# Mixture-of-experts tiles moved between the attention rounds of later blocks

## The chip, the cores and the metric

The kernel runs on one core of a Trainium2 chip. The metric is device time in microseconds (us): the median of three runs. One further execution was taken with the hardware profiler; all views below are of that execution.

## What is computed

The input is 16 sequences of 256 tokens of width 128, in float32. Four residual layers follow each other: causal attention with 16 heads of width 8, a mixture of experts, a second attention (no mask, another scaling of the scores), and the same mixture of experts again.

```python
x = x + attn_a(layernorm(x))
x = x + ffn(layernorm(x))
x = x + attn_b(layernorm(x))
x = x + ffn(layernorm(x))

def ffn(x):                       # 8 experts, 2 per token, hidden width 512
    top_vals, top_idx = top_k(x @ Wr, 2)
    rw = softmax(top_vals)
    combine = sum(rw[..., None] * one_hot(top_idx, 8))
    h = silu(x @ Wg[e]) * (x @ Wu[e])
    eo = (h @ Wd[e]) / sqrt(12)
    return sum over e of combine[:, e] * eo[:, e]
```

Both attentions take a softmax over the keys, so they need exponentials; the experts need a SiLU.

## The kernel before

**Two attentions, each followed by its experts.** The 4096 tokens are cut into 8 blocks of 512 tokens (two sequences of 256). `attention` goes over 128 rounds. A round is one block, one sequence of it, and one of 8 pairs of head groups: two heads at a time. At round `at` the loop emits, in this order: the scores of that round with queries on the partitions (`rows_scores`), the exponentials of the round 14 rounds back (`exponentials`: the scores again with keys on the partitions, then Exp on ScalarE, and for the causal layer a POOL select on the diagonal), the mask and the row maxima (`rows_maxima`: one VectorE reduction), and every second round the product with the values of the round 17 back (`values`). The maxima are transposed and laid into two spare rows of q by a DMA (`lay_maxima`), so that the second scores come out with the maximum subtracted.

**Everything else is cut into tasks.** `project` (layer norm, q, k, v of a block), `collect` (division by the sum), `finish` (output projection and residual) and `route` are generators. At each `yield` a task names in how many rounds it wants to go on and what it needs: `BANK` (the one PSUM bank for small products, tag `mm`), `BUSY` (a busy engine) or `FREE`. `later` and `due` give out at most one or two such steps after each round. All engine calls of this part go through `InOrder`, which keeps the program order on each engine.

**Routing.** `route` takes a finished block, normalizes it, computes the expert logits, finds the best two, counts with two small matmuls which place each token gets in its expert's region of the DRAM table `rows_in` (`free` carries the counts from block to block), and scatters each token's row twice with 8 indirect DMAs from POOL, one per round. A row is 128 values, the token's number and its weight.

**Experts.** After the last block `tiles_of` turns the counts into a list of 39 tiles of 256 rows (expert number and first row each), `pads` fills the open end of each region with 8 DMAs, and `experts` runs over the 39 tiles. The order of this part is left to the scheduler. A tile loads its rows and three weight matrices (`fetch`, 0.9 MB, all on SP's queue), transposes the rows, and in four steps of 128 hidden units multiplies by Wg and Wu, takes Silu on ScalarE and the product on VectorE; then it multiplies by Wd (`down`), scales by the token's weight, and adds the 256 result rows to DRAM sums with two indirect DMAs from POOL that accumulate (`finish`). The adds alternate between two sums, and adds to one sum follow one another. Tokens of a tile that do not exist are sent to a spare row. After the second layer the two sums are loaded, added and stored.

**Buffers.** q and k have three buffers of a whole block each (`qs`, `ks`), v has three with 32 columns per head of which 9 are used. PSUM has 8 banks: in attention three pairs for the scores (`psum_s`), one for the values and one for small products.

The lines that set the pace of the experts' stage:

```python
    experts("a", attention(weights_a, True, "a"), totals[0], False)
    experts("b", attention(weights_b, False, "b"), totals[1], True)
```

Of the kernel before, what the change touches and what calls it, by code (L numbers as in the profile page):

```python
# [32 lines left out]
F32 = mybir.dt.float32  # L34
# [8 lines left out]
P = 128  # L43
NH = 16
# [12 lines left out]
SEQ = 256  # L57
EPS = 1e-5
# [4 lines left out]
TOKENS = 4096  # L63
W = P + 2
# [6 lines left out]
def layers(  # L71
# [23 lines left out]
    ot = out.flatten_outer_dims().rearrange("(n t p) d -> n p t d", t=NT, p=P)  # L95
# [18 lines left out]
    def attention_weights(wq, bq, wk, bk, wv, bv, wo, bo, scale, name):  # L114
# [27 lines left out]
    blocks = ctx.enter_context(tc.tile_pool(name="blocks", bufs=4))  # L142
# [17 lines left out]
    half = const.tile([P, NE], F32, name="half")  # L160
# [14 lines left out]
    tokens = const.tile([P, NB * NT], F32, name="tokens")  # L175
    within = tokens[:, 0:ET]
    nobody = const.tile([P, 1], F32, name="nobody")
# [4 lines left out]
    totals = [  # L182
        [dram.tile([TOKENS + P, P], F32, name=f"total{i}{j}") for j in range(2)] for i in range(2)
    ]
    blank = const.tile([P, 3 * W], F32, name="blank")
    wr_sb = const.tile([P, NE], F32, name="wr_sb")

    def zeros():

        yield sy.dma_start(  # L190
            out=rows_in[NE * CAP : NE * CAP + TE, :].rearrange("(s p) d -> p s d", p=P),
            in_=blank[:, 0 : ET * W].rearrange("p (s d) -> p s d", s=ET),
        )
        for first, second in totals:
            flat = second.rearrange("(p a m) d -> p a (m d)", p=P, m=3)
            for k, m in ((0, 4), (4, 8), (8, 11)):
                to = flat[:, k:m, :]
                yield sy.dma_start(
                    out=to,
                    in_=blank[:, 0 : 3 * P].unsqueeze(1).to_broadcast([P, to.shape[1], 3 * P]),  # L200
                )
            yield sy.dma_start(out=first[TOKENS : TOKENS + P, :], in_=blank[:, 0:P])

    slots = [const.tile([P, 2, NT], I32, name=f"slots{n}") for n in range(NB)]

    vs = [const.tile([P, NT, NH, HS], F32, name=f"v{i}") for i in range(3)]
    qs = [const.tile([P, NP, TB], F32R, name=f"q{i}") for i in range(3)]
    ks = [const.tile([P, NP, TB], F32R, name=f"k{i}") for i in range(3)]
# [30 lines left out]
    def later_constants():  # L239
# [19 lines left out]
        for t, pattern, base, by_partition in (  # L259
# [4 lines left out]
            (tokens, [[P, NB * NT]], 0, 1),  # L264
            (nobody, [[0, 1]], TOKENS, 1),
# [8 lines left out]
    def prepared(i):  # L274

        for t in (ks, qs) if i else ():
            for g in range(0, NP, 4):
                po.memset(t[i].bitcast(F32)[:, g : g + 4, :], 0.0)
                yield 1, FREE
        for j in range(2):  # L280
            row = j * HP + TOP
            sy.dma_start(
                out=ks[i].bitcast(F32)[row : row + 2, :, :].rearrange("p g (a m) -> p (g a) m", m=P),
                in_=ones[0:2, :].unsqueeze(1).to_broadcast([2, NP * NT, P]),
            )
        po.memset(vs[i], 0.0)
        po.memset(vs[i].rearrange("p t h r -> p (t h) r")[:, :, 0:1], 1.0)
# [44 lines left out]
    def route(pool, psum, n, xb, free, sent):  # L332
# [4 lines left out]
        yield 1, BUSY  # L337
# [6 lines left out]
            tokens[:, n * NT : (n + 1) * NT].unsqueeze(1).to_broadcast([P, 2, NT]),  # L344
# [54 lines left out]
        ve.tensor_tensor(w2, share[:, 1], w1, ALU.mult)  # L399
        for t in range(NT):  # L400
            for s in range(2):
# [6 lines left out]
                tc.declare_no_dep(scatter.ins, group=sent[0], reason="no row is written twice")  # L408
                tc.add_to_no_dep_group(sent[0], scatter.ins)
                sent.append(scatter)  # L410

    def tiles_of(pool, free):

        count = pool.tile([P, NE], F32, tag="count")
        nc.vector.tensor_tensor(count, free, regions, ALU.subtract)
        more = pool.tile([P, NE, CAP // TE], F32, tag="more")
        nc.vector.tensor_tensor(
            more, count.unsqueeze(2).to_broadcast([P, NE, CAP // TE]), steps, ALU.is_gt  # L420
        )
        need = pool.tile([P, NE], F32, tag="need")
        nc.vector.tensor_reduce(need, more, AX.X, ALU.add)
        sums_to = pool.tile([P, NE, NE], F32, tag="sums_to")
        nc.vector.tensor_tensor(
            sums_to, need.unsqueeze(1).to_broadcast([P, NE, NE]), upto, ALU.mult
        )
        end = pool.tile([P, NE], F32, tag="end")
        nc.vector.tensor_reduce(end, sums_to, AX.X, ALU.add)
        wide = [P, TILES, NE]  # L430

        past = pool.tile([P, TILES, NE + 1], F32, tag="past")
        nc.vector.memset(past[:, :, 0:1], 1.0)
        nc.vector.tensor_tensor(
            past[:, :, 1:], numbers.unsqueeze(2).to_broadcast(wide),
            end.unsqueeze(1).to_broadcast(wide), ALU.is_ge,
        )
        expert = pool.tile([P, TILES], F32, tag="expert")
        nc.vector.tensor_reduce(expert, past[:, :, 1:], AX.X, ALU.add)
        mine = pool.tile(wide, F32, tag="mine")  # L440
        nc.vector.tensor_tensor(mine, past[:, :, 1:], need.unsqueeze(1).to_broadcast(wide), ALU.mult)
        skipped = pool.tile([P, TILES], F32, tag="skipped")
        nc.vector.tensor_reduce(skipped, mine, AX.X, ALU.add)
        nc.vector.tensor_tensor(skipped, numbers, skipped, ALU.subtract)
        nc.vector.tensor_scalar_mul(skipped, skipped, float(TE))
        first = pool.tile([P, TILES], F32, tag="first")
        nc.vector.scalar_tensor_tensor(first, expert, float(CAP), skipped, ALU.mult, ALU.add)

        nc.vector.tensor_scalar_min(first, first, float(NE * CAP))
        table = pool.tile([P, 2, TILES], I32, tag="table")  # L450
        nc.vector.tensor_scalar_min(table[:, 0, :], expert, float(NE - 1))
        nc.vector.tensor_copy(table[:, 1, :], first)
        nc.vector.tensor_tensor(mine, past[:, :, 0:NE], past[:, :, 1:], ALU.subtract)
        nc.vector.tensor_tensor(mine, mine, free.unsqueeze(1).to_broadcast(wide), ALU.mult)
        left = pool.tile([P, TILES], F32, tag="left")
        nc.vector.tensor_reduce(left, mine, AX.X, ALU.add)
        nc.vector.tensor_tensor(left, left, first, ALU.subtract)
        return table, left
# [7 lines left out]
    def pads(free, sent):  # L466

        ends = tables.tile([P, NE], I32, tag="ends")
        ve.tensor_copy(ends, free)
        for e in range(NE):  # L470
            r = number(ends[0:1, e : e + 1], e * CAP + TOKENS)
            pad = sy.dma_start(
                out=rows_in[bass.ds(r, TE), :].rearrange("(s p) d -> p s d", p=P),
                in_=blank[:, 0 : ET * W].rearrange("p (s d) -> p s d", s=ET),
            )
            tc.declare_no_dep(pad.ins, group=sent[0], reason="no row is written twice")
            tc.add_to_no_dep_group(sent[0], pad.ins)
            sent.append(pad)

    def tokens_of(total, n):  # L480
        return total[n * TB : (n + 1) * TB, :].rearrange("(t p) d -> p t d", p=P)
# [27 lines left out]
    def attention(w, causal, name):  # L509
        with ExitStack() as own:  # L510
            pool = own.enter_context(tc.tile_pool(name=f"att_{name}", bufs=2))
            psum = own.enter_context(tc.tile_pool(name=f"att_{name}_mm", bufs=1, space=PSUM))
            psum_s = own.enter_context(tc.tile_pool(name=f"att_{name}_s", bufs=3, space=PSUM))
# [8 lines left out]
            def loaded(n):  # L522
# [5 lines left out]
                sy.dma_start(out=xb, in_=xt[n] if causal else tokens_of(totals[0][0], n))  # L528
                xs[n] = xb
                if not causal:  # L530
                    more = pool.tile([P, NT, P], F32, tag="more", bufs=1)
                    sy.dma_start(out=more, in_=tokens_of(totals[0][1], n))
                    return more

            def project(n):
# [38 lines left out]
                lay(ks[n % 3], halves(k, "k"), (0, 2, 1, 3))  # L574
                if causal:
                    yield 2, BANK
                    q = biased("wq", "bq", "q")
                    lay(qs[n % 3], halves(q, "q"), (0, 1, 2, 3), se if n == 0 else sy)
                else:
# [14 lines left out]
                    lay(qs[n % 3], (hi, lo), (0, 1, 2, 3), se if n == 0 else sy)  # L594
# [20 lines left out]
            def lay(to, parts, order, queue=sy):  # L615

                for i, slot in enumerate(order):
                    queue.dma_start(  # L620
                        out=to.bitcast(F32)[slot : slot + P - SLOTS + 1 : SLOTS, :, :],
                        in_=parts[i // 2].bitcast(F32),
                    )
# [9 lines left out]
            def scales(n, q, k, junk):  # L633
# [38 lines left out]
                po.tensor_tensor(den, den, half[:, 0:2], ALU.pow)  # L672
# [35 lines left out]
            def rows_scores(n, b, g):  # L708

                q, k = qs[n % 3], ks[n % 3]  # L710
                s = psum_s.tile([P, 2, TB], F32, tag="s")
                for t in range(2):
                    keys = P * (t + 1) if causal else SEQ
                    at = (P if causal else SEQ) * t
                    for j in range(2):
# [3 lines left out]
                            lhsT=q[r, g, b * SEQ + t * P : b * SEQ + (t + 1) * P],  # L719
                            rhs=k[r, g, b * SEQ : b * SEQ + keys],  # L720
# [395 lines left out]
```

## Time and profile before

| | us |
|---|---|
| median of three runs (1350.26 to 1352.62) | 1352.59 |
| the profiled execution: its own time | 1343.86 |
| the profiled execution: span from first to last instruction | 1342.2 |

| stage of the profiled execution | from, us | to, us |
|---|---|---|
| attention a, up to the last row scores | 0 | 353 |
| drain of attention a | 353 | 422.5 |
| experts a | 422.5 | 647 |
| start of attention b | 647 | 690 |
| attention b, up to the last row scores | 690 | 1021 |
| drain of attention b | 1021 | 1087 |
| experts b | 1087 | 1310 |
| output | 1310 | 1342 |

Busy time and share of the span: PE (TensorE matmuls) 1066.8 us (79%), DVE (VectorE) 787.6 (59%), ACT (ScalarE) 518.8 (39%), POOL (GpSimd) 594.0 (44%). The mean granted TensorE clock is 0.872 of full speed.

How to read it: one digit of a slice row is the busy share of 1/40 of the span in tenths. A row of a table by stage gives, after the stretch and its length, the busy time of each engine with its number of instructions, the granted clock, the share of the DMA engines, and GB/s. A row of the timeline gives start, duration, engine, line, operation with output and inputs, count, and in brackets the engine's idle time before it and what ended that. A busy PE is not PE at its peak[...]. Where `InOrder` records an instruction, its line is 222, whatever function issued it.

### The profile page before, as it was taken

The numbers are of one execution on the slowest core, as the hardware profiler recorded it, in microseconds if no ns is written. First come the engines' busy times: TensorE is split into PE (matmuls) and PEld (weight loads), VectorE is DVE, ScalarE is ACT, GpSimd is POOL, SyncE is SP. The second block draws the span as 40 slices with busy tenths as digits, with TensorE's granted clock in tenths as the row PEclk, the third lists the DMA queues.
The fourth block names the chain that finished last, engine by engine and source line by source line (L and its number), as shares of the span: only waits on it lengthen the run. The fifth ranks groups of instructions, "written<-read, shape, count | busy, mean of one in ns | idle before, by whom it ended". The sixth has DMA issues, their size and how long they took to land. (4 is left out here: it accounts for less than half of the span.)

```text
span 1342.2 us, 23350 instructions
## 1 busy us (share of the span) xinstructions
PE 1066.8 (79%) x8116; PEld 771.8 (58%) x8116; DVE 787.6 (59%) x2221; ACT 518.8 (39%) x942; POOL 594.0 (44%) x599
## 2 busy tenths in 40 slices
PE   2799888898763999999457888778877459999990
PEld 1455555555543888888324454445554248888880
DVE  3667667776533555454258787888675535554541
ACT  1156445554521222222135756665555212222220
POOL 7444546655552555555330114233323325555551
PEclk9889878888855999999757999998788779999995
DMA  4244324530015877776253324133300087777757
GB/s 98 51 97 109 72 73 117 138 84 24 25 36 169 210 188 189 180 195 133 45 109 81 66 58 104 51 78 83 89 23 30 27 230 192 178 187 189 189 103 195
DMA packets 175301, 150.84 MB, mean 112 GB/s; under 512 B 14286, under 2 KB 136784, under 8 KB 175184
## 3 DMA queue, kind: packets, MB, share of 16 engines
q1 hardware_dynamic: 145310, 127.18, 34.8%
q0 software_dynamic: 26560, 18.76, 9.4%
q10 hardware_dynamic: 3314, 3.41, 1.1%
q8 instruction: 65, 1.06, 0.3%
q14 instruction: 52, 0.43, 0.1%
HBM read 82.74 MB, written 31.75 MB: 85 GB/s over the span
## 5 line engine op out<-in xcount | busy, mean ns | idle before, releaser
L1019 POOL DMA_INDIRECT total<-y,to x156 | 242.8, 1556 | 229.2 <-DVE here L1005 59.3
L222 DVE TENSOR_REDUCE mx<-s 128x6 f32<-128x768 f32 (+1 forms) x256 | 277.1, 1084 | 110.4 <-PE s L222 109.4
L222 ACT ACTIVATE p<-s 128x768 f32<-128x768 f32 (+1 forms) x256 | 232.9, 916 | 192.2 <-PE s L222 170.2
L1061 ACT ACTIVATE sg<-pg 128x256 f32<-128x256 f32 x312 | 119.4, 383 | 316.8 <-PE pg L1049 300.7
L1063 DVE TENSOR_TENSOR h<-pu,sg 128x256 f32<-128x256 f32 x312 | 131.9, 423 | 149.6 <-PE pu L1053 147.2
L222 POOL DMA_INDIRECT rows_in<-both_rows,slots x128 | 128.9, 1007 | 172.2 <-DVE both_rows L222 113.0
L1053 PE MATMUL pu<-xT,w_u 128*128 128x256 f32 x624 | 190.2, 387 | 5.7 <-DVE h L1063 5.5
L1049 PE MATMUL pg<-xT,w_g 128*128 128x256 f32 x624 | 192.6, 391 | 1.2 <-DMA w_g<-in_L_ffn_Wg_dram 0.7
L1028 PEld LDWEIGHTS py<-w_d,h 128*128 128x128 f32 x1248 | 163.8, 192 | 8.1
L1028 PE MATMUL py<-w_d,h 128*128 128x128 f32 x1248 | 164.6, 275 | 0.0
L222 PE MATMUL s<-k,q 62*128 62x256 f32 (+1 forms) x1024 | 144.3, 367 | 16.1 <-DMA k<-lo 11.4
L222 PE MATMUL s<-q,k 64*128 64x256 f32 (+1 forms) x1024 | 114.2, 307 | 42.1 <-DVE mx L222 33.5
L222 PE MATMUL av<-p,v 128*32 128x256 f32 (+1 forms) x2048 | 144.5, 406 | 0.3 <-ACT au L222 0.2
L222 PEld LDWEIGHTS s<-k,q 62*128 62x128 f32 x1024 | 89.2, 216 | 87.7 <-issue 51.8
L1053 PEld LDWEIGHTS pu<-xT,w_u 128*128 128x128 f32 x624 | 118.0, 192 | 29.6 <-DVE h L1063 13.8
L222 POOL TENSOR_SCALAR_AFFINE_SELECT p<-p 128x512 f32<-128x512 f32 x128 | 82.5, 645 | 108.3 <-ACT p L222 103.7
L222 PEld LDWEIGHTS s<-q,k 64*128 64x128 f32 x1024 | 89.5, 213 | 58.9 <-DVE mx L222 39.7
L1049 PEld LDWEIGHTS pg<-xT,w_g 128*128 128x128 f32 x624 | 102.2, 194 | 20.3 <-issue 13.8
L222 PEld LDWEIGHTS av<-p,v 128*32 128x32 f32 x2048 | 58.7, 120 | 55.2 <-issue 26.4
L222 POOL TENSOR_TENSOR lo<-to,hi 128x512 fp32r<-128x512 f32 x24 | 30.6, 1273 | 72.4 <-ACT hi L222 72.3
L996 PE MATMUL ps<-ident,x_in 128*128 128x128 f32 x156 | 30.6, 279 | 39.1 <-DMA x_in<-rows_in 39.1
L222 PE MATMUL s<-mask_q,ident_h 128*128 128x256 bf16 x256 | 58.6, 317 | 0.0
(206 smaller groups left out, 1179.3 us busy)
## 6 DMA issues: line engine op xcount, KB each, us to landing
w_g<-in_L_ffn_Wg_dram SPq DMA_DIRECT2D x78, 256.0 KB
w_u<-in_L_ffn_Wu_dram SPq DMA_DIRECT2D x78, 256.0 KB
w_d<-in_L_ffn_Wd_dram SPq DMA_DIRECT2D x78, 256.0 KB
x_in<-rows_in SPq DMA_DIRECT2D x78, 130.0 KB
k<-hi SPq DMA_DIRECT2D x32, 256.0 KB
k<-lo SPq DMA_DIRECT2D x32, 256.0 KB
q<-hi SPq DMA_DIRECT2D x28, 256.0 KB
q<-lo SPq DMA_DIRECT2D x28, 256.0 KB
```

Of the source, the lines that this page charges most:

```text
L222: return tc.keep_in_program_order(method(*args, **kwargs))
L996: nc.tensor.transpose(ps[:, bass.ts(s, P)], x_in[:, s, 0:P], ident)
L1019: nc.gpsimd.indirect_dma_start(out=sums[(i * ET + s) % 2], out_offset=bass.IndirectOffsetOnAxis(ap=to[:, s : s + 1], axis=0), in_=y[:, s, ...
L1028: nc.tensor.matmul(py[:, s, :], lhsT=hs[c][:, bass.ts(s, P)], rhs=w_d[:, c, :], start=c == 0, stop=c == NC - 1,)
L1049: nc.tensor.matmul(pg, lhsT=w_g[:, bass.ts(c, P)], rhs=this, start=True, stop=True)
L1053: nc.tensor.matmul(pu, lhsT=w_u[:, bass.ts(c, P)], rhs=this, start=True, stop=True)
L1061: nc.scalar.activation(sg, pg, AF.Silu)
L1063: nc.vector.tensor_tensor(h, pu, sg, ALU.mult)
```

## The change

A class `Mixture` replaces `tiles_of`, `pads` and `experts`. After each block's routing, `choose` works out which experts now have a full tile of 256 rows that was not computed yet. With 8 experts, at least `sure(n)` such tiles exist after block n, whatever the routing: 0, 1, 5, 9, 13, 17, 21 for blocks 0 to 6. They are admitted two rounds after the block's last scatter; the last block admits the remaining 18 of the 39.

`Mixture.step` is called once in every round of attention, just ahead of `due`. It emits at most one quarter of a tile (`part`: one Wg and one Wu product, in two of four quarters half of the previous tile's `down`, one Silu, one product), one addition of finished rows, and a `fetch` when fewer than two tiles are loaded. What is left when the rounds are over is done by `rest`, one tile after the other. All of it is in program order now.

With it come these changes:

- PSUM: two pairs for the scores instead of three, one bank for a quarter's two products (`psum_gu`), one for the down product; `rest` has four banks for the quarters.
- The copy of a tile's transposed rows and the scaling of its result go from VectorE to ScalarE.
- q and k are kept by sequence: four buffers of 256 columns each (`RING`), filled by separate DMAs for each half of a block. v has 9 columns per head; the values' PSUM tile is kept and cleared once.
- A row carries its target: token number for the first choice, token number plus 4096 for the second. One DRAM tensor per layer holds two sums, no row is added to twice in one of them, and the adds are declared free of order among each other (`unordered`). The attention's residual is stored into the first sum; loads that need all rows wait for the scatters or adds by name (`wait_for`).
- `route` pauses three rounds, not one, between the moments and the normalization.
- The final sums are read and stored with 2 KB per partition, on the queues of SP and ACT in turn.

```diff
+RING = 4
+    psum = ctx.enter_context(tc.tile_pool(name="mm", bufs=1, space=PSUM))
+    psum_y = ctx.enter_context(tc.tile_pool(name="y", bufs=1, space=PSUM))
+    psum_gu = ctx.enter_context(tc.tile_pool(name="gu", bufs=1, space=PSUM))
...
-    vs = [const.tile([P, NT, NH, HS], F32, name=f"v{i}") for i in range(3)]
-    qs = [const.tile([P, NP, TB], F32R, name=f"q{i}") for i in range(3)]
-    ks = [const.tile([P, NP, TB], F32R, name=f"k{i}") for i in range(3)]
+    vs = [const.tile([P, NT, NH, 1 + HD], F32, name=f"v{i}") for i in range(3)]
+    qs = [const.tile([P, NP, SEQ], F32R, name=f"q{i}") for i in range(RING)]
+    ks = [const.tile([P, NP, SEQ], F32R, name=f"k{i}") for i in range(RING)]
...
         mv, rstd = yield from moments(pool, xb)
-        yield 1, BUSY
+        yield 3, BUSY
...
+    def sure(n):
+        return max(0, -(-(2 * TB * (n + 1) - NE * (TE - 1)) // TE))
...
+        def part(self, bank):
+            tile = self.now
+            c = tile["c"]
+            gu = bank.tile([P, 2, TE], F32, tag="gu")
+            for i, k in enumerate(("w_g", "w_u")):
+                te.matmul(
+                    gu[:, i, :], lhsT=tile[k][:, bass.ts(c, P)], rhs=tile["xT"], start=True, stop=True
+                )
+            if c > 0 and self.before is not None:
+                self.down()
+            sg = ffn.tile([P, TE], F32, tag="sg")
+            se.activation(sg, gu[:, 0, :], AF.Silu)
+            h = ffn.tile([P, TE], F32, tag="h", bufs=2 * NC)
+            ve.tensor_tensor(h, gu[:, 1, :], sg, ALU.mult)
...
+            y = ffn.tile([P, P], F32, tag="y_out", bufs=6)
+            se.activation(
+                y, py[:, s, :], AF.Identity, scale=tile["x_in"][:, s, P + 1 : P + 2]
+            )
...
+        def step(self, at, later):
+            if self.out:
+                self.add()
+            if self.now is None and self.loaded and "xT" in self.loaded[0]:
+                self.now = self.loaded.pop(0)
+            if self.now is not None:
+                self.part(psum_gu)
+            elif self.before is not None:
+                self.down()
+            if self.known and len(self.loaded) < 2:
+                self.fetch()
+                self.loaded[-1]["from"] = at + 3
+            if self.loaded and self.loaded[0].get("from", at + 1) <= at:
+                if self.now is None or self.now["c"] > 1:
+                    del self.loaded[0]["from"]
+                    later(1, BANK, turned(self, self.loaded[0]), 0)
...
-            psum_s = own.enter_context(tc.tile_pool(name=f"att_{name}_s", bufs=3, space=PSUM))
+            psum_s = own.enter_context(tc.tile_pool(name=f"att_{name}_s", bufs=2, space=PSUM))
...
                         task = collect(m, c, e, av, outs[m])
                         later(*next(task), task)
+                mixture.step(at, later)
                 due()
                 at += 1
...
+    landed = ()
+    for i, w in enumerate((weights_a, weights_b)):
+        name = "ab"[i]
+        mixture = Mixture(name, totals[i])
+        attention(w, i == 0, name, mixture, landed)
+        with tc.tile_pool(name=f"gu_{name}", bufs=4, space=PSUM) as bank:
+            mixture.rest(bank)
+        landed = mixture.added
+    outputs(mixture)
```

## Prediction

> **What bounds the kernel now.** I read the page's slices first, then a table of busy time by stage, then what ScalarE (ACT) does at the stage borders.
>
> ```profile
> span 1342.2 us, 23350 instructions
> PE   2799888898763999999457888778877459999990
> ACT  1156445554521222222135756665555212222220
> PEclk9889878888855999999757999998788779999995
> ```
>
> The slices show two equal halves: an attention stage (PE 7 to 9, granted clock dipping to 7 or 8), a dip, an experts' stage (PE 9, clock 9). By stage:
>
> ```profile
> core 0: us, PE busy (x) PEld busy (x) DVE busy (x) ACT busy (x) POOL busy (x), PEclk, DMA share, GB/s
> 294.00:353.00 59.00, 51.00 (x499) 32.46 (x490) 38.05 (x98) 26.95 (x40) 34.16 (x47) 0.83 0.14 38
> 353.00:422.50 69.50, 32.77 (x296) 22.48 (x296) 29.86 (x141) 18.14 (x30) 36.98 (x46) 0.63 0.18 51
> 422.50:647.00 224.50, 220.74 (x1326) 195.20 (x1326) 113.48 (x348) 60.97 (x157) 116.70 (x76) 0.98 0.74 181
> 946.00:1021.00 75.00, 61.52 (x575) 38.32 (x575) 55.03 (x135) 42.54 (x61) 22.30 (x25) 0.82 0.20 52
> 1021.00:1087.00 66.00, 27.95 (x269) 17.09 (x265) 27.00 (x132) 20.00 (x29) 26.71 (x30) 0.75 0.18 53
> 1087.00:1310.00 223.00, 219.78 (x1325) 193.87 (x1326) 113.38 (x348) 60.98 (x157) 116.81 (x75) 0.99 0.74 183
> ```
>
> See three things. The experts are PE-bound (220.7 of 224.5 us; 39 tiles, 5.7 us each). The drains (353 to 422 and 1021 to 1087), from the last scores of an attention to its first expert tile, keep PE busy under half of the time: that is what the change fills. In full attention ACT is busy for only 27 of 59 us. What decides is what ACT pays to go from attention to experts:
>
> ```profile
> 422.51 0.66 PE L996 MATMUL ps<-ident,x_in 128*128 128x128 f32 x2 [20.01 <-DMA x_in<-rows_in]
> ...
> 425.06 1.28 ACT L1061 ACT_TABLE_LOAD   x1 [22.60 <-PE pg L1049]
> 426.36 0.69 ACT L1061 ACTIVATE sg<-pg 128x256 f32<-128x256 f32 x2
> ...
> 709.52 0.66 ACT L222 COPY v<-pv 128x512 f32<-128x512 f32 x1 [2.17 <-PE pv L222]
> 710.20 1.28 ACT L222 ACT_TABLE_LOAD   x1
> ```
>
> Exp (attention) and Silu (experts) do not share a function table: the first Silu after the Exps costs a load of 1.28 us, and so does the way back. The gaps beside it are 0.02 us (709.52+0.66 to 710.20; 425.06+1.28 to 426.36), so 1.30 us each. Before has 4 loads in all.
>
> **The change in the order of instructions.** The built order of ACT has 168 table loads, 83 up to the end of the first layer's experts and 85 after. Each round of attention that carries a quarter of a tile holds Exp, load, Silu, load. Counting PE's order, quarters lie in rounds 88 to 91 and 104 to 127 of layer a, and 86 to 89 and 104 to 127 of layer b; 11 and 14 more beside the last Exps; 19 and 19 in the last block's routing; 99 and 97 after it.
>
> Rounds in time: the mask has 2 matmuls per round, and 176, 32 and 46 records lie before 250, 294 and 353 us, so rounds 88, 104 and 127 stand there. In layer b the row maxima (1.23 us each) put round 85 at about 901, 104 at 959, 128 at 1021.
>
> **Layer a, rounds 104 to 127.** ACT's list, by durations of before: 44 loads x 1.30 = 57.2; 23 Exp x 0.81 = 18.6; 22 Silu x 0.385 = 8.5; 10 y evacuations, new on ACT, near the 0.27 us copy of 128x128, 0.3 each = 3; 5 xT copies at 0.4 = 2; 5 au x 0.586 = 2.9; 6 DMA issues x 0.64 = 3.8; other copies 5. Sum 101 us. PE's list, by warm start-to-start distances: 23 x (scores 0.33 + 0.33, mask 0.32, half of 0.79 values) = 31; 22 gate-and-up pairs x 0.85 = 19; 10 downs x 0.89 = 9; transposes 2; block work (projections, transposes, routing, output) 9.9 per block = 14. Sum 75. ACT is the longer by 26 us, so the stage is ACT-bound: 101 and some 5 for waits in order, 106 against 59: **+47**. The 4 rounds at 88 the same way, 4.5 instead of 2.75 us: **+7**.
>
> **Layer a, drain.** Beside the last 15 Exps ACT has 23 loads (30), Exps 12, Silus 4, the rest 9: 55, with waits 57 us; PE has 34. Then the last routing with 19 quarters: PE 19 x 0.85 + 8 x 0.89 + 8 of its own = 31, say 33. Together 90 against 69.5: **+20**. The 20 us in which PE waited for the last rows are covered: 27 quarters of sure tiles (38 us) stand between the last routing's matmuls and the last tiles.
>
> **Layer a, rest.** 99 pairs x 0.85 + 52 downs x 0.89 + 24 transposes x 0.43 = 140, with 6 for the stricter order (xT and y now on ACT) 146, against 224.5: **-78**.
>
> **Layer a, earlier.** Two score buffers instead of three: by the order's waits, a round's scores wait for the Exp before them; mask and values (0.3 to 1.1 us on PE) cover most of an Exp's 0.81; bounds 0 and +20, taken **+6**. The new pause of three rounds after the moments takes away a wait of DVE for POOL's rstd (2.15 us at 257, then PE 2.94 us idle, then half clock for some 4 us): 4 blocks x 4 us, bounds 0 and -30, taken **-16**. The new table of sure tiles: some 15 DVE operations of 0.2 us per block, **+3**. Laying q and k by sequence lets the first round start on half of the data (PE waits 11.4 us for k there): **-4**; cost of doubled issues (0.6 us each on SP and ACT) is beside that, and for later blocks they stand some 10 rounds ahead. Waiting costs in order, lumped: **+4**. Layer a: 47+7+20-78+6-16+3-4+4 = **-11**.
>
> **Layer b.** Rounds 104 to 127: 42 loads = 55, 23 Exps x 1.02 = 23.5, the rest 26: 104, with waits 111 against 62: **+49**. Four rounds at 86: **+7**. Drain: 29 loads (38), Exps 15, Silus 5, rest 10: 68, with waits 72, and routing 36: 108 against 66: **+42**. Rest: 97 pairs, 50 downs, 23 transposes: 137, with waits 142 against 223: **-81**. Two buffers cost more here, as no mask stands between: Exp 1.02, 0.25 to and fro, two score groups of 0.43 make 2.13 us before any other ACT work, against 2.5 us now: bounds 0 and +40, taken **+20**. DVE (55 of 75 busy) feels the table: **+6**; rstd **-3** (POOL is idle here); start **-2**. Layer b: **+38**.
>
> **Costed at nothing.** POOL's additions (2 x 1.56 us per tile) lie beside its idle time (it is busy for 34 of 59 and 22 of 75 us); unordered, they no longer wait for one another, but PE was not waiting for them (220.7 of 224.5 us busy). Weights in attention: 0.9 MB per four rounds (18 us), 50 GB/s beside 38 to 52. SP: each fetch waits for scatters sent five rounds before, and q and k lie behind it with ten rounds in hand; if that cover is gone, each late landing costs 3 us a block. The narrower v (9 columns, still in its 32-column place) changes no matmul. **Output:** 22 us at DMA share 0.93 with rows of 512 bytes; rows of 2 KB and two queues: **-4** (bounds 0 and -8).
>
> **Sum.** -11 + 38 - 4 = +23 on the profiled execution's 1343.86. The median of the runs, 1352.59, is 8.7 above it; the same step gives **1376 us**.
>
> **Rules of the skill.** The trace says 1.30 us for a switch. The Trainium skill, "ScalarE: Activation LUTs", section "What ACT_TABLE_LOAD costs", gives the same 1283 ns for the load, but adds a drain of about 1380 ns, 2.66 us for every switch, and tells one to batch calls by table set: it speaks against this change. By its figure the 164 added loads cost 436 us of ACT instead of 213, and some 200 us more would be on the path: 1575. I take the trace, as no gap beside its loads is longer than 0.02 us, though none of the three stands directly behind a matmul-fed Exp. For the clock: after PE's idle stretch near 170 us the windows show 0.50. "TensorE: Matmul & The Clock Gate", section "HAM oscillation", puts the limit at idle gaps of some 3 us; in ACT-bound rounds PE idles about 1.1 us a round, so I cost the parts at full clock; at the 0.82 of today PE's 75 us would be 91, still under ACT's 101.
>
> **Rivals.**
> 1. *Faster: the waits of rounds 0 to 104 close.* The loads cost what I say, but the two score buffers cost nothing (-26), and the longer pause recovers the 9 us per block that layer a loses today (44 us a block, of which PE's warm work is 32), 5 more for each of 4 blocks, and 2 in b (-28): 1322. It decides from 23 us saved there. For it: PE's gaps do follow DVE's wait for rstd. Against: POOL is 3.6 of 4 us busy in those gaps, and in b it is not. Chance 0.20.
> 2. *Faster: ACT is not the bound* (a table set with both functions, or loads that hide). Then rounds 104 to 127 and the drains are PE's: -26-17 in a, -30-28 in b: 1275. The built order shows the loads, so 0.07.
> 3. *Slower by far: the drain of each switch is paid*: 1575, chance 0.06.
> 4. My forecast, ACT-bound rounds at 4.4 to 4.8 us, 1376: 0.62; its own range 1345 to 1415. No change: 0.05.
>
> A measurement of this kernel can tell about 0.2% (2.7 us) from no change. Faster 0.27, same 0.05, slower 0.68. The range goes down to 1322, where rival 1 lies, and up to 1428 (my forecast with the 2-buffer cost at its upper end and 5% more waits in ACT's list); outside it lie rival 2, rival 3 and a few in a hundred more.
>
> **What would show it.** ACT busy near 730 us (519 + 213) with about 168 loads of 1.28 us; in the rounds with quarters ACT above 90% busy at 4.4 to 5 us a round, PE near 75%; drains without the 20 us wait; rests of about 146 and 142 us. Wrong, if those rounds take under 3.6 us, if ACT idles beside its loads, if the gap before an Exp's load is over 1 us (then rival 3), or if rounds 0 to 86 move by over 20 us in either layer.

## The result, and the profile after

The changed kernel takes 1532.3 us (median of 4 runs, 1530.6 to 1533.8), the kernel before 1351.7 (4 runs on the same chip): a ratio of 1.134, interval [1.132, 1.136]. Slower, as forecast, but by 181 us, not by 23. The profiled execution spans 1532.1 us against 1342.2.

The page of the changed kernel: the slices, the chain that ended last, and three groups (busy time and mean ns of one, then the idle time before them and what ended most of it).

```profile
span 1532.1 us, 23853 instructions
...
PE   4887888777877677997577777787667667769992
...
ACT  1454447486887323442344554564788986213441
...
PEclk9897899897888969999568776887999888879996
...
PE 51%; ACT 19%; DVE 15%; issue 8%; DMA 3%; POOL 2%; ACTq 1%; another core or an unknown queue 0%; SPq 0%; POOLq 0%; DVEq 0%
...
L229 DVE TENSOR_TENSOR h<-gu,sg 128x256 f32<-128x256 f32 x312 | 132.4, 424 | 498.7 <-ACT sg L229 471.9
...
L229 PE MATMUL gu<-xT,w_g 128*128 128x256 f32 x624 | 223.6, 443 | 123.7 <-DVE h L229 107.8
L229 ACT ACT_TABLE_LOAD x168 | 215.5, 1283 | 26.6 <-issue 12.0
```

The 168 loads are there, each as long as forecast. New is the other group: gate and up wait 107.8 us for `h`, the product of the quarter before, and the chain that ended last passes from PE (51% of the span) to ACT (19%) and DVE (15%). The long rows of 9 in PE's slices have shrunk, but what stands in front of them is a row of 6 and 7 where before there was a short dip.

A row by stage, each stage cut at the row maxima and Exps (columns: start:end, length, then busy time and instructions of PE, PEld, DVE, ACT and POOL, the granted clock, DMA share, GB/s):

```profile
core 0: us, PE busy (x) PEld busy (x) DVE busy (x) ACT busy (x) POOL busy (x), PEclk, DMA share, GB/s
309.00:429.00 120.00, 94.21 (x676) 66.66 (x675) 48.07 (x143) 96.26 (x123) 44.21 (x50) 0.82 0.29 72
429.00:489.00 60.00, 43.93 (x303) 32.12 (x307) 18.69 (x87) 50.63 (x65) 31.63 (x34) 0.82 0.28 64
489.00:597.00 108.00, 73.79 (x360) 56.81 (x353) 36.83 (x172) 30.03 (x72) 43.09 (x36) 0.84 0.44 105
597.00:713.00 116.00, 116.00 (x703) 102.32 (x702) 40.23 (x121) 47.32 (x143) 62.40 (x41) 1.00 0.75 175
759.00:1020.00 261.00, 200.61 (x1499) 115.18 (x1495) 176.89 (x451) 132.19 (x226) 51.95 (x57) 0.75 0.23 64
1092.80:1210.20 117.40, 86.45 (x651) 59.18 (x651) 59.60 (x169) 102.07 (x124) 29.40 (x27) 0.90 0.28 69
```

Rounds 0 to 85 of layer b in the kernel before:

```profile
691.00:906.00 215.00, 168.40 (x1502) 102.05 (x1498) 175.38 (x439) 131.23 (x225) 55.34 (x60) 0.89 0.32 76
```

Three stages carry the loss. Rounds 104 to 127 (309 to 429, and 1093 to 1210 in layer b; 23 rounds from maximum to maximum) take 5.2 and 5.1 us each, with ACT busy for 80 and 87%. After the last Exps (489 to 597) neither PE (74 of 108) nor ACT (30 of 108) is full: something else sets the pace. And rounds 0 to 85 of layer b (759 to 1020), nearly all without any tile, take 261 us where the kernel before took 215 (691 to 906): PE is busy for 201 us against 168 there, with 1499 matmuls recorded against 1502, at a granted clock of 0.75 instead of 0.89.

What each stage took in the profiled executions, with the main experiments, whose edits stand below, beside them ("rounds": first to last row maximum; "Exps": to the end of the last Exp; "experts": to the first maximum of layer b, or to the end):

| us | before | changed | e3 | e4 | e13 | e15 | e8 | e14 |
|---|---|---|---|---|---|---|---|---|
| a: rounds | 324 | 402 | 357 | 334 | 365 | 390 | 286 | 288 |
| a: Exps | 26 | 61 | 26 | 30 | 41 | 59 | 27 | 27 |
| a: experts | 311 | 269 | 313 | 314 | 240 | 231 | 298 | 298 |
| b: rounds | 329 | 451 | 387 | 409 | 420 | 441 | 352 | 332 |
| b: Exps | 27 | 70 | 30 | 30 | 43 | 64 | 31 | 27 |
| b: experts, output | 295 | 252 | 298 | 297 | 214 | 212 | 282 | 274 |

### The profile page after: what moved, and what is told of

It is laid out like the page before. It is cut to its first block, busy times and chain, and to the rows that moved or that the text cites. A ratio compares the mean times of both kernels' runs of the same rounds, so it can differ in the third digit from the quotient of the medians.

```text
span 1532.1 us, 23853 instructions
## 1 busy us (share of the span) xinstructions
PE 1167.8 (76%) x8116; PEld 813.2 (53%) x8116; DVE 733.6 (48%) x2204; ACT 792.4 (52%) x1340; POOL 581.9 (38%) x595
## 4 chain that ended last, share of the span: by engine, by line
PE 51%; ACT 19%; DVE 15%; issue 8%; DMA 3%; POOL 2%; ACTq 1%; another core or an unknown queue 0%; SPq 0%; POOLq 0%; DVEq 0%
PE gu L229 18%; PE ps L229 9%; PE y L229 9%; PE s L229 8%; ACT L229 7%; DVE mx L229 5%; PE av L229 5%; ACT p L229 4%; ACT sg L229 3%; DVE h L229 2%; PE pv L229 1%; ACT y L229 1%; DVE xn L229 1%; ACT to L229 1%; ACTq L229 1%
## 5 line engine op out<-in xcount | busy, mean ns | idle before, releaser
L229 DVE TENSOR_TENSOR h<-gu,sg 128x256 f32<-128x256 f32 x312 | 132.4, 424 | 498.7 <-ACT sg L229 471.9
L229 PE MATMUL gu<-xT,w_g 128*128 128x256 f32 x624 | 223.6, 443 | 123.7 <-DVE h L229 107.8
L229 PE MATMUL gu<-xT,w_u 128*128 128x256 f32 x624 | 203.1, 410 | 0.0
L229 PEld LDWEIGHTS gu<-xT,w_g 128*128 128x128 f32 x624 | 103.8, 203 | 186.1 <-DVE h L229 141.1
L229 PEld LDWEIGHTS y<-w_d,h 128*128 128x128 f32 x1248 | 180.4, 209 | 18.6 <-DVE h L229 5.5
L229 PE MATMUL y<-w_d,h 128*128 128x128 f32 x1248 | 183.1, 293 | 5.5 <-DVE h L229 4.1
L229 ACT ACTIVATE y<-y,x_in 128x128 f32<-128x128 f32 x156 | 57.3, 368 | 233.9 <-PE y L229 178.9
L229 ACT ACTIVATE sg<-gu 128x256 f32<-128x256 f32 x312 | 118.9, 381 | 92.4 <-PE gu L229 91.0
L229 PE MATMUL av<-p,v 128*9 128x256 f32 (+1 forms) x2048 | 152.9, 426 | 0.0
L229 PEld LDWEIGHTS gu<-xT,w_u 128*128 128x128 f32 x624 | 129.9, 208 | 20.9
```

The lines of the kernel that those rows point to most:

```text
L229: return tc.keep_in_program_order(method(*args, **kwargs))
```

## The experiments

Medians are given, and the ratio to the kernel before on the same chip (1356 to 1357 us there) with its interval.

### The loads: what they hold up

**e1_tanh**: the gate's SiLU from Tanh, no change of table.

```
-            se.activation(sg, gu[:, 0, :], AF.Silu)
-            ve.tensor_tensor(h, gu[:, 1, :], sg, ALU.mult)
+            se.activation(sg, gu[:, 0, :], AF.Tanh, scale=0.5)
+            ve.scalar_tensor_tensor(sg, sg, 1.0, gu[:, 0, :], ALU.add, ALU.mult)
+            ve.scalar_tensor_tensor(h, sg, 0.5, gu[:, 1, :], ALU.mult, ALU.mult)
```

> Edit: the gate's SiLU is formed from Tanh, which lies in Exp's table set (h = 0.5 * (1 + tanh(g/2)) * g * u; one more 128x256 operation on DVE per quarter): 1 table load instead of 168, everything else as in the changed kernel. Theory A (my forecast: the loads fill ACT in the rounds): rounds with quarters fall from 5 us to what PE needs, about 3.3 us, so some 38 rounds x 1.7 = 65 us per layer are won; the stretch after the last Exps (500 to 600 and 1290 to 1390 us in the changed kernel) has no loads and gets some 0.4 us per quarter longer, 46 quarters, +19 us per layer: 1532 - 130 + 38 = 1440. Theory B (the one bank for gate and up, in which quarter k+1 waits for quarter k's SiLU and product, limits everywhere, loads or not): rounds stay above 4.5 us, total 1530 to 1570.

Measured: 1471.5 us (1.086 [1.079, 1.092]), 61 less. Rounds: 402 to 363 us in layer a, 451 to 425 in b; the Exps 61 to 43 and 70 to 48. The experts' part got longer, 269 to 292 and 252 to 268: all of it in the quarters through the one bank, where the further DVE operation lengthens every turn (from the 81st quarter on, with four banks, a quarter takes 1.41 us in both kernels). Theory A is borne out in the rounds, theory B after them; neither is enough.

The loads on ACT's timeline in the changed kernel, layer b (start, duration):

```profile
1199.77 1.02 ACT L229 ACTIVATE p<-s 128x1024 f32<-128x1024 f32 x1
1200.81 1.28 ACT L229 ACT_TABLE_LOAD   x1
1202.11 0.38 ACT L229 ACTIVATE sg<-gu 128x256 f32<-128x256 f32 x1
1202.51 1.28 ACT L229 ACT_TABLE_LOAD   x1
1203.80 1.02 ACT L229 ACTIVATE p<-s 128x1024 f32<-128x1024 f32 x1
```

Exp, load, SiLU, load fill 4.03 us without a hole: from the end of a matmul-fed Exp to the load behind it 0.02 us (1199.77 + 1.02 to 1200.81). It is 0.02 us in all 35 places of this profile where a load stands directly behind an Exp.

### The chain after the last Exps

The timeline of the changed kernel at 523 us; in the brackets, the idle time before and what ended it:

```profile
522.84 0.70 PE L229 MATMUL gu<-xT,w_g 128*128 128x256 f32 x2 [0.93 <-DVE h L229]
...
523.38 0.59 PE L229 MATMUL gu<-xT,w_u 128*128 128x256 f32 x2
...
524.01 0.38 ACT L229 ACTIVATE sg<-gu 128x256 f32<-128x256 f32 x1 [1.68 <-PE gu L229]
524.42 0.42 DVE L229 TENSOR_TENSOR h<-gu,sg 128x256 f32<-128x256 f32 x1 [0.83 <-ACT sg L229]
...
524.90 0.70 PE L229 MATMUL gu<-xT,w_g 128*128 128x256 f32 x2 [0.93 <-DVE h L229]
...
525.87 1.05 PE L229 MATMUL y<-w_d,h 128*128 128x128 f32 x8
526.96 0.37 ACT L229 ACTIVATE y<-y,x_in 128x128 f32<-128x128 f32 x1 [2.57 <-PE y L229]
527.23 0.38 ACT L229 ACTIVATE sg<-gu 128x256 f32<-128x256 f32 x1
...
527.63 0.43 DVE L229 TENSOR_TENSOR h<-gu,sg 128x256 f32<-128x256 f32 x1 [2.71 <-ACT sg L229]
...
528.12 0.70 PE L229 MATMUL gu<-xT,w_g 128*128 128x256 f32 x2 [1.19 <-DVE h L229]
```

Three engines take turns. There is one gate-and-up bank (`psum_gu`, `bufs=1`), so the next quarter's matmuls wait until `h` has read it: 522.84 to 524.90, 2.06 us a quarter, although PE needs 0.85. In a quarter with a down, SiLU stands on ACT behind the evacuation of `y`, which waits for the down: 524.90 to 528.12, 3.22 us. A tile of two such pairs costs 10.6 us here, 5.7 in the kernel before. No table load is in sight.

**e2_two_gate_banks**: `psum_gu` with two banks, the down through the block work's bank.

```
-    psum_y = ctx.enter_context(tc.tile_pool(name="y", bufs=1, space=PSUM))
-    psum_gu = ctx.enter_context(tc.tile_pool(name="gu", bufs=1, space=PSUM))
+    psum_gu = ctx.enter_context(tc.tile_pool(name="gu", bufs=2, space=PSUM))
...
-            py = tile["py"]
+            py = psum.tile([P, P], F32, tag="mm", name="y")
```

> Edit: gate and up get two PSUM banks instead of one, the down product goes through the block work's bank instead of its own; 168 loads stay. Theory B (one bank makes PE wait for SiLU and product of the quarter before, 2.07 us a quarter without and 3.2 us with a down, seen after the last Exps): that stretch falls from some 95 us to some 65 per layer, 4 x 0.85 + 2 x 0.89 = 5.2 us a tile plus the routing's own work; in the rounds with quarters ACT stays the limit and they win at most 0.3 us each: total 1532 - 60 - 20 = 1450. Theory A alone (loads only): no change beyond 10 us, 1525 to 1540.

1492.2 us (1.097 [1.090, 1.104]): 40 less, half of what was expected; the down now shares a bank with all block work, which may be why, but was not tested. The rounds did not move (402 and 457).

**e5_score_banks_after_exps**: gate and up in the score buffers once those are free.

```
+                gu = scores.tile([P, 2, TB], F32, tag="s", name="gu")
+                gu = gu[:, 0, :].rearrange("p (i e) -> p i e", i=2)
...
-                mixture.step(at, later)
+                mixture.step(at, later, psum_s if at >= len(rounds) + lag else None)
```

> The changed kernel, but from the round after the last Exp on (attention round 142) gate and up are written into the two score buffers, which are free by then, instead of into the one bank of their own; down and block work keep their banks; 168 table loads stay. Theory B (after the last Exps PE waits for the SiLU and product of the quarter before, 2.07 or 3.2 us a quarter): some 36 quarters a layer fall to about 1.5 us: 1532 - 2 x 36 x 1.1 = 1450. Rival (in that stretch the order of the routing, the transfers or the clock set the pace): 1515 to 1535.

1471.6 us (1.087 [1.079, 1.095]), 61 less where 82 were expected; the experts' parts 269 to 238 and 252 to 222. PE's waits after the last Exps (us in total, times, longest), in the changed kernel:

```profile
PE gu L229 <- DVE h L229: 26.9, 25, 2.6
```

and with the score banks:

```profile
PE gu L229 <- DVE h L229: 3.6, 3, 2.0
```

**e9_silu_ahead_of_down**: one bank, one order turned.

```
-            if c > 0 and self.before is not None:
-                self.down()
             sg = ffn.tile([P, TE], F32, tag="sg")
...
             ve.tensor_tensor(h, gu[:, 1, :], sg, ALU.mult)
             tile["h"].append(h)
+            if c > 0 and self.before is not None:
+                self.down()
```

> The changed kernel with one order turned: SiLU and product of a quarter are issued ahead of the down product's evacuation, so that on ACT SiLU no longer stands behind y; the one bank stays, 168 loads stay. Theory B: every second quarter after the last Exps falls from 3.2 to about 2.1 us, 18 x 1.1 = 20 us a layer, and in the rounds with quarters ACT stops waiting for y with Exp's table loaded and SiLU still to come (some 12 rounds a layer x 1 us): 1532 - 40 - 24 = 1468. Rival as above: 1520 to 1535.

1460.7 us (1.082 [1.073, 1.091]): 72 less from the place of two lines. 24 and 26 us come from the experts' parts, the rest mostly from the rounds and last Exps with quarters. Rounds 104 to 127 fall from 120 to 107 us in layer a, but only from 117 to 116 in b.

**e13_changed_without_both** and **e15_changed_loads_only**: the order turned and the score banks used, with Tanh (4 loads) and with SiLU (168 loads).

> The changed kernel (two score buffers, quarters in the attention's rounds) with loads and chain taken away together: Tanh for SiLU in the loop (4 loads), SiLU and product ahead of the down's evacuation, score banks for gate and up after the last Exps. The parts alone took off 61, 72 and 61 us, the last two of one stretch: together about 61 + 85 = 146, so 1386. If loads and chain are the whole cost of the interleave, it stands 50 us below the no-interleave kernel (1435), and what keeps it above the kernel before are the two score buffers (+82). Rival (a quarter in a round costs PE more than it saves later): above 1420.

> The changed kernel with the chain taken away (SiLU and product ahead of the down's evacuation, score banks after the last Exps) and the 168 loads kept, SiLU itself in the loop: beside the kernel without both (1343) it gives the loads' own price with no chain beside it. Theory A (ACT is filled by Exp, load, SiLU, load: 2.6 us a round in 38 rounds of each layer, less what PE needs): 1343 + 2 x 38 x 1.3 = 1440. Rival (with the chain gone the loads hide beside PE's work): below 1380. In the changed kernel the order turned alone gave 1461; if the loads and the chain only hurt together, this is near 1380 too.

e13: 1343.0 us (20 runs, 0.993 [0.990, 0.995]), e15: 1429.1 (6 runs, 1425 to 1434; the kernel before lay at 1334 to 1369 beside it, so no interval). So, with the chain taken away first, the chain cost 1532 - 1429 = 103 us and the loads 1429 - 1343 = 86; with the loads taken away first (e1) it is 61 for the loads and 1471.5 - 1343 = 128 for the chain. Both Tanh kernels pay for a further DVE operation, so the loads' figures are net of that. Layer a's rounds 104 to 127 in e15, then in e13:

```profile
310.00:416.00 106.00, 83.87 (x670) 59.17 (x672) 47.33 (x141) 95.03 (x120) 42.45 (x50) 0.90 0.32 81
```

```profile
311.00:391.00 80.00, 74.09 (x660) 54.17 (x660) 59.52 (x165) 38.96 (x78) 42.87 (x50) 0.98 0.43 107
```

and layer b's in e15:

```profile
1030.80:1147.20 116.40, 87.82 (x639) 60.32 (x640) 60.69 (x169) 101.71 (x124) 29.40 (x27) 0.87 0.28 70
```

With the chain gone and the loads kept, layer a takes 106 us with ACT busy for 95, and b 116 with ACT busy for 102; without loads a takes 80 us with PE busy for 74, and b 93. In layer b these rounds take as long in e15 as in the changed kernel (117): there the loads alone set them, and the chain costs nothing. My expectation for e13 was 43 us too high: it had the loads at e1's 61 and the chain at 85. Taken away alone, each gives less, since what one frees the other still holds; in e1 Tanh's further operation even lengthened the chain.

### Two score buffers

**e3_before_two_score_buffers**: the kernel before, `psum_s` with `bufs=2` instead of 3.

> The kernel before with two score buffers instead of three, nothing else. Theory C (the two buffers are what slows layer b's rounds 0 to 85 from 2.48 to 3.0 us in the changed kernel): layer b's attention +60 us over 128 rounds, layer a +10, total 1352 + 70 = 1422. Rival (something else does: the queues, the layout by sequence, POOL): at most my forecast's 26, total under 1380.

1438.8 us (1.059 [1.053, 1.065]): 82 us slower by this alone, 33 in layer a's rounds and 58 in b's. Rounds 16 to 96 of layer b in the kernel before, with PE's two waits for score buffers (us in total, times, longest):

```profile
721.00:936.00 215.00, 173.94 (x1613) 104.05 (x1613) 172.29 (x453) 138.75 (x230) 59.53 (x66) 0.93 0.32 76
```

```profile
PE s L222 <- DVE mx L222: 7.6, 8, 1.8
...
PE s L222 <- ACT p L222: 3.8, 8, 2.0
```

and in e3:

```profile
759.00:1020.00 261.00, 207.45 (x1612) 123.76 (x1611) 174.81 (x453) 138.85 (x226) 59.23 (x66) 0.78 0.26 63
```

```profile
PE s L222 <- DVE mx L222: 25.0, 26, 2.3
PE s L222 <- ACT p L222: 13.2, 14, 2.4
```

The waits for score buffers grow from 11 to 38 us, most of them for the row maximum. Other waits of PE, for the block work, get shorter, so that its idle time grows only from 41 to 54 us. The larger part of the 46 us is PE's busy time, 207 instead of 174 us for the same matmuls, at a granted clock of 0.78 instead of 0.93. That the missing buffer lowers the clock is shown, as nothing else was changed (over the whole kernel it is 0.825 to 0.835 in four runs, and 0.865 to 0.876 in seven of the kernel before); how is not. All of PE's stops over 0.15 us together are 54 instead of 46 in a longer stretch, and the longest is 2.4 us instead of 2.2.

**e4_no_interleave**: the changed kernel, with `step` returning at once, so that all 39 tiles run in the rest.

> The changed kernel, but no tile is computed before the attention is over: all 39 tiles run in the rest, as before (the sure tiles' tables get 8 buffers instead of 2). 4 table loads. It prices all other parts of the change together. Theory C: rounds of layer b as slow as in the changed kernel (+60), layer a near before, drains as before: 1352 + 65 = 1417. Rival (rounds 0 to 85 of layer b are slow because of quarters' work elsewhere, so not here): about 1350 to 1365.

1435.6 us (1.056 [1.050, 1.062]). All that is not the interleave costs 78 us, and the buffers alone cost 82 on the kernel before, so the other parts together come to about nothing. The interleave adds 97 to that: 103 for the chain and 86 for the loads, less a gain of 92, which e13 shows bare (1343 against 1435.6). Even bare, the gain does little more than pay for the buffers.

### What the table and the pause cost

**e7_three_buffers_no_round_quarters**: three score buffers, no quarter before the last Exp, then in the score buffers.

```
-name=f"att_{name}_s", bufs=2, space=PSUM
+name=f"att_{name}_s", bufs=3, space=PSUM
...
-                mixture.step(at, later)
+                if at >= len(rounds) + lag:
+                    mixture.step(at, later, in_scores)
```

> The changed kernel with three score buffers again; the bank of gate and up and that of y are given up for it, quarters are computed only after the last Exp, in the score buffers, and none in the attention's rounds; 8 table loads. Theory: three buffers give back 33 us in layer a and 58 in b (as the kernel before loses with two), which puts the no-interleave kernel's 1435 at 1344; filling the stretch between the last Exps and the last rows (about 40 us of PE at half use before) with 28 quarters of 1.4 us a layer takes off 20 to 35 a layer: 1275 to 1305, faster than the kernel before. Rival (the 2-buffer cost and the rest overlap, or the routing's own chain sets that stretch): 1340 to 1360.

1326.7 us (0.981 [0.974, 0.988]): about 2% faster than the kernel before, but over 20 us short of what was expected, as the experts' parts fell only to 292 and 275.

**e8_late_table**: and the table made after blocks 5 and 6 only.

```
-        return max(0, -(-(2 * TB * (n + 1) - NE * (TE - 1)) // TE))
+        return max(0, -(-(2 * TB * (n + 1) - NE * (TE - 1)) // TE)) if n > 4 else 0
```

> The kernel with three buffers and no quarters in the rounds, and the sure tiles' table is made only after blocks 5 and 6 of each layer (16 and 5 tiles) instead of after seven blocks. Theory D (layer b's rounds 80 to 127 are 20 us longer in the no-interleave kernel than in the kernel before with two buffers, because the table's 16 VectorE operations stand among the maxima): 15 to 25 us less than the kernel with three buffers and tables after every block. Rival (another part of the change makes them longer: the layout by sequence, the pause of three rounds): within 6 us of it.

1305.2 us (three runs, 1302.6 to 1311.4; 0.967 [0.958, 0.977]); a fourth run took 3157 us, for a reason that nothing here shows, and is left out (with it the median is 1308.3, from which the later expectations start). That is 22 less than e7, as theory D said; but the rounds that got shorter are mainly layer a's (306 to 286, b 360 to 352), and the intervals of the two overlap.

**e12_late_table_short_pause** and **e14_long_pause_in_a_only**: e8 with `yield 1` instead of `yield 3` after the moments in both layers; then in layer b alone.

> The late-table kernel with the routing's pause after the moments at one round, as in the kernel before, instead of three. My forecast put the longer pause at -16 us in layer a and -3 in b: this kernel would take 1308 + 19 = 1327, with layer a's rounds 64 to 127 longer by some 15. Rival (the gain of layer a lies in the layout by sequence or elsewhere): 1303 to 1313.

> The late-table kernel with the routing's pause of three rounds in layer a and one round in layer b. In the kernels with one and with three rounds, layer a's 128 rounds took 314 and 286 us, layer b's 341 and 352, and the stretch from the last Exp to the end of b 274 and 283. If these are the pause's own effects, this kernel takes layer a from the one and layer b from the other: 1308 - 20 = 1288, or less if b's stretch after the Exps keeps the gain of the short pause: 1270 to 1290. Rival (the differences are the clock's scatter between runs): 1300 to 1312.

e12: 1296.0 us (0.961 [0.953, 0.970]), not slower as expected. Layer a's rounds did get longer, 286 to 315, but b's got shorter (352 to 341), and so did both experts' parts. e14: 1281.2 us (6 runs, 1270 to 1285; the kernel before at 1334 to 1369 beside it, so no interval), with a's rounds at 288 and b's at 332. So the longer pause is a gain in layer a and a loss in b, for reasons that were not traced, and e14 is the fastest kernel here.

**e10_late_table_silu_first** (e8 with e9's order) and **e11_tanh_beside_last_exps** (e10 with quarters from round 128 on, through Tanh, and a third table).

> The late-table kernel (three score buffers, quarters only after the last Exps, table after blocks 5 and 6) with SiLU and product issued ahead of the down's evacuation, in the loop and in the rest. With three score banks and four gate banks PE should not wait for SiLU in order: theory B says the order was worth 72 us only because of the one bank, so here 0 to 8 us: 1300 to 1308. Rival (ACT's order matters by itself): 20 us or more.

> The kernel before this one, and quarters from round 128 on, beside the last 14 Exps, with the gate's SiLU formed from Tanh in the loop (no load there), the table made after blocks 4, 5 and 6; 41 quarters a layer in the loop instead of 25. PE is busy for about half of the 25 us between the last maxima and the last Exp, so some 8 to 9 quarters of 1.43 us fit: 12 us a layer less, the added table +3 a layer: 1285. Rival (three buffers shared by Exps and quarters make them wait for one another, as with two): 1300 to 1320.

e10: 1310.8 us (0.971 [0.965, 0.977]), no faster than e8: with enough banks the order is worth nothing. e11: 1354.8 us (1.000 [0.997, 1.004]), a miss by 70 us. The Exps' tails grew by 11 and 15 us, and the experts' parts, with 16 quarters a layer fewer to do, did not shrink (303 against 301 us in a). The profiles show where: the last row of the routing is scattered 98 us after the last Exp in layer a instead of 74 (e10), and up to there PE waits 28 us for `h` instead of 13. SiLU from Tanh takes two operations of DVE, which the routing needs too; that this is the cause was not tested.

## Why the forecast was wrong in size

The difference of the two profiled spans, by stages, against the same terms of the sum:

| stage | forecast, us | measured, us |
|---|---|---|
| a: start, rounds 0 to 103 | 0 | +12 |
| a: rounds 104 to 127 | +47 | +63 |
| a: to the last Exp | +31 | +35 |
| a: to layer b's first maximum | -91 | -42 |
| b: rounds 0 to 103 | +30 | +64 |
| b: rounds 104 to 127 | +49 | +58 |
| b: to the last Exp | +46 | +44 |
| b: to the end | -89 | -44 |
| sum | +23 | +190 |

**The step that failed first: "The last routing with 19 quarters ... 33 us" and "rest 146".** Both were sums of PE's work. The bank was in the diff (`psum_gu`, `bufs=1`), and I counted the down's order as "6 for the stricter order". Following one quarter through PE, ACT, DVE and back would have given 2 and 3 us instead of 1.4. Measured: the routing with its 19 quarters took 65 us (in b 61, forecast 36), and the rest 163 (164, forecast 142). Within the rest only the first 15 or so were slow, which still went through the one bank while the routing's last rows were scattered; I had costed them like the others. From the 81st quarter on, with four banks, one took 1.41 us, as costed. So the two experts' parts fell by 86 us in all instead of by 180; 94 of the 167 us missed lie here. With the chain removed (e15) they fell by 163: the sum of PE's work was nearly right as a lower bound.

**The second: two score buffers, "bounds 0 and +20" and "0 and +40".** Measured alone (e3): +33 and +58, outside both bounds. I let a round's scores wait for the Exp before them, and weighed ACT's occupancy. I left out the row maximum, which holds a score buffer too: 25 of the 38 us that PE waits for buffers in e3 are for it. And I put the clock at nothing: I had costed "the parts at full clock" because PE idles only 1.1 us at a time, but of e3's 46 us in rounds 16 to 96 of layer b, 33 are PE's busy time at 0.78 instead of 0.93. The limit of some 3 us does not describe this case: with no stop of PE over 2.2 us the kernel before has stretches at 0.50 there (802 to 811 us, for one), and e3 stops for 2.4 us at most. The Trainium skill, "TensorE: Matmul & The Clock Gate", section "A second HAM failure mode: psum-queue depth-cycling", tells of a kernel whose matmuls cycle through PSUM banks and whose frequent short stops make the clock swing; e3 is nearer to that, though its stops are hardly more frequent than before, so what lowers the clock stays open.

**Right: the loads make the rounds with quarters ACT-bound.** 101 us of ACT's list and 106 of time were forecast for layer a; with only the loads kept (e15) ACT is busy for 95 of 106 us. In the changed kernel the stage took 120, and the difference is the order of `y` and SiLU, which alone (e9) brings it to 107: ACT was at 80%, not above 90, and a round at 5.2 us. (In all ACT was busy for 792 us, not 730: that sign added the loads alone and left out the work moved to ACT, of which `y` is 57.) Layer b: 111 forecast, 116 in e15, 117 measured. So the direction came out as forecast in part for the forecast reason, but these loads alone would not have given +190.

**Right in sign in layer a only: the pause** (-16 and -3 us). On e8's base it gave -29 us in layer a's rounds and +11 in b's, and with the parts behind them the long pause in both layers came out 9 us slower than the short one (1305 against 1296, with overlapping intervals). And the table, at +3 and +6, cost more like 20 and 8 (e7 to e8, near the scatter between runs).

**The rivals.** Rival 1 (1322, faster) fell with the two buffers, its first premise. Rival 2 (ACT not the bound) fell with the loads' 86 us. Rival 3 named the time that came nearest, 1575, for a reason that isn't there: the load follows a matmul-fed Exp after 0.02 us, 35 times out of 35. Against the 1.38 us of drain that the Trainium skill adds ("ScalarE: Activation LUTs", section "What ACT_TABLE_LOAD costs"), the measurement decides: a switch cost 1.30 us of ACT here. (The same page's rule to batch calls by set, which the prediction quotes with it, stands in the section "Table sets: the hidden batching unit".) A near number is no evidence for a mechanism.

**What would show it wrong**: I had written "if rounds 0 to 86 move by over 20 us in either layer". Layer b's moved by 46, and that pointed to e3.

## What to carry to other kernels

When work of a second kind is put between the steps of a pipeline, cost it as a loop, not as a sum: follow one unit through every engine back to the buffer it frees, and take the longer of that loop and the engine's work. A PSUM buffer taken from the running pipeline has a price of its own (82 us here for the third score buffer), so test it alone on the old kernel first. Functions that alternate should share a table set (Tanh with Exp, here), and of two operations on one in-order engine, the one that frees the bank which the next matmul waits for goes first (72 us for two lines).

## What the hardware showed that I had not expected

- A switch of function tables behind a matmul-fed Exp costs its load of 1.28 us and a gap of 0.02 us. Of the 213 us of added loads, 61 reached the span while the chain stood beside them and 86 without it.
- Taking one score buffer away costs more in PE's own time than in its waits: 1612 matmuls took 207 instead of 174 us at a granted clock of 0.78 instead of 0.93, while PE's idle time went from 41 to 54 us and no stop was longer than 2.4.
- In e13 rounds 104 to 127, with quarters between them, ran at a granted clock of 0.98 (layer a) and 0.92 (b), where the kernel before had 0.83 and 0.82: part of the added work was paid by the clock. PE's busy share alone does not set it: it was 93 and 84% in e13, 86 and 82% in the kernel before, and in the changed kernel layer b had the higher clock (0.90 against 0.82) at the lower share (74 against 79%).
